# Four states of a selective scan through TensorE in the first three sequences, instead of two

## The chip, the cores and the metric

The kernel runs on one core of one Trainium2 chip. The metric is the device time of one execution, in microseconds (us). A core has five engines that run side by side and wait for each other by semaphores: TensorE (PE; its weight loads are listed as PEld), VectorE (DVE), ScalarE (ACT), GpSimd (POOL) and SyncE (SP), which here only issues DMAs. ACT also issues some DMAs.

## The reference

Sixteen sequences of 512 positions and 256 features go through a bidirectional state-space layer with a residual and a layer norm, and then through a soft mixture of 16 experts with a residual and a layer norm. The part that matters here is the scan. Per sequence and direction, with 512 channels and 16 states:

```
dA  = dt * A                      # per channel and state
dBu = dt * u * B                  # B: one value per position and state
xs  = recurrence h[t] = exp(dA[t]) * h[t-1] + dBu[t], with a gate for the reference's 1e-12
y   = sum over states of xs * C   # C: one value per position and state
y   = y + u * D, times silu(res)
```

The backward direction runs over the positions in reverse. `dt` is a softplus of a projection of `u`, and `B` and `C` are projections of `u` as well.

## The kernel before

**Layout.** Channels lie on the 128 partitions, in four chunks of 128, and the 512 positions along the free dimension. All is in fp32. For each sequence `b` the scan is done in four calls of `scan_part(b, r, p, ...)`: pair 0 of the chunks forward (`r` = 0) and backward (`r` = 1), then pair 1 forward and backward. I call these calls parts. Three sequences make twelve parts, numbered 0 to 11.

**One part** loops over the 16 states two at a time (`n` = 0, 2, ..., 14) and in it over the two chunks of the pair. That makes 16 steps, each with two states of one chunk. In a step:

- POOL multiplies `du` = dt*u with the broadcast rows `bs` of B into `db` (L427), for both states at once: 128 x 1024.
- ACT makes the decay exp(dt*A) into `h` in PSUM (L444) and a tanh gate `th` (L446), one of each per state.
- DVE runs the recurrence, one `tensor_tensor_scan` per state (L450 forward, L452 backward), and multiplies with the gate into `hg` (L455).
- POOL multiplies `hg` with the broadcast rows `cs` of C (L456), again 128 x 1024.
- PE adds `hg` into the accumulator `acc` in PSUM by matmuls with the identity (L371, in `add_up`), two steps late. `hg` has four buffers, `db`, `bs` and `cs` have three.

**Diagonal states.** For the two states in `DIAG` = (5, 13) the product dt*u*B is not made by POOL. PE makes it as a matmul of the transposed `du` (`duT`, turned by PE and copied by ACT in `turn_pair`, L350 and L355) with a matrix `dg` that has the row of B on its diagonal (L405, in `by_diagonal`). It issues four 128x128 matmuls per state and chunk, into a PSUM bank `hd`, one step ahead of the scan that reads it. In such a step `db` is only 128 x 512 (`k` = 1), half of `bs` is loaded, and the decay of the diagonal state goes to `dec` in SBUF.

**Where the diagonal matrices come from.** `diag_dram` holds one matrix per direction, diagonal state and group of 128 positions, in rows of P+1 elements, so that column 0 of that view is the diagonal. At the start the whole of it is zeroed from an SBUF tile `blank`, by DMAs on ACT's queue (L188). In `project_unit`, when `xd` (which holds the rows of B and C) is there, one DMA on ACT's queue writes the diagonal elements of the direction's states, one by one (L297). `scan_part` then loads `dg` (L420, one buffer) on SP's queue, two states (one `n`) before its first use.

**Order around the scan.** SP's queue carries `bs` (L416), `cs` (L417), `dg`, the inputs and the weights, in one order. Beside the scan three lists of generators, `prep`, `front` and `back`, emit other work: the projections of the next direction or sequence, the layer norm and the expert routing of the sequence before, and from sequence 3 on also the experts. `beside_scan` gives each of them at most a piece per step, as long as the PSUM banks in use (three of tag `mps`, of which a held `hd` takes one) allow it. The order on each engine is fixed when the program is built, partly by a scheduler and partly by `late`, which keeps an instruction at its place. The constants of the later stages are loaded by `constants`, called once after the first `prep_forward`.

Of the kernel before, what the change touches and what calls it, by code (L numbers as in the profile page):

```python
# [9 lines left out]
F32 = mybir.dt.float32  # L10
# [7 lines left out]
P = 128  # L18
L = 512
NL = L // P  # L20
# [4 lines left out]
NS = 16  # L25
DTR = 16
XB, XC = 32, 64
XW = XC + NS
KW = 4
NE = 16  # L30
DIAG = (5, 13)
DIAG_SIZE = P * (P + 1)
SL = 64
NSL = NE * SL
# [21 lines left out]
def seq_layers(tc, ident, neghalf, a, out):  # L56
# [20 lines left out]
    nc = tc.nc  # L77
    nb = a["x"].shape[0]
    with ExitStack() as ctx:
        drams = ctx.enter_context(tc.tile_pool(name="drams", bufs=1, space=DRAM))  # L80
# [2 lines left out]
        s_dram = drams.tile([nb, NM, P, NSL], F32, name="s_dram")  # L83
        e_dram = drams.tile([NE, nb * SL, DM], F32, name="e_dram")

        diag_dram = drams.tile([2, len(DIAG), NL, DIAG_SIZE], F32, name="diag_dram")
        const = ctx.enter_context(tc.tile_pool(name="m_const", bufs=1))
        p1 = ctx.enter_context(tc.tile_pool(name="m_p1", bufs=1))
        p2 = ctx.enter_context(tc.tile_pool(name="m_p2", bufs=2))
# [53 lines left out]
        side = [{}, {}]  # L143
# [14 lines left out]
        def steps(w, s, m):  # L158
            w["dtT"] = const.tile([DTR + 1, DI], F32, name=f"dtT_{s}")
            nc.sync.dma_start(w["dtT"][:DTR, :], a[f"dt_proj{m}T"])  # L160
            nc.sync.dma_start(w["dtT"][DTR : DTR + 1, :], a[f"dt_proj{m}_b"].unsqueeze(0))
            w["A"] = const.tile([P, ND, NS], F32, name=f"A_{s}")
            nc.sync.dma_start(w["A"], a[f"A{m}_log"].rearrange("(c p) n -> p c n", p=P))
            d = channels(a[f"D{m}"], f"D_{s}")
            w["diagD"] = const.tile([P, ND, P], F32, name=f"diagD_{s}")
            for c in range(ND):
                late(nc.vector.tensor_scalar(w["diagD"][:, c, :], ident, d[:, c : c + 1], None, ALU.mult))
# [5 lines left out]
            nc.vector.tensor_scalar(w["Ah"], w["A"], 0.5, None, ALU.mult)  # L173

        def constants():
            steps(side[0], "f", "")
            projections(side[1], "b", "_b")
            steps(side[1], "b", "_b")
            outT = const.tile([P, ND, DM], F32, name="outT")
            nc.sync.dma_start(outT, a["out_projT"].rearrange("(c p) o -> p c o", p=P))  # L180
            late(nc.vector.tensor_scalar(outT, outT, 0.5, None, ALU.mult))
            return outT

        projections(side[0], "f", "")
        blank = p2.tile([P, 4 * DM], F32, tag="W", name="blank", bufs=3)
        nc.vector.memset(blank, 0.0)
        for part in diag_dram.rearrange("r i l (p s) -> (r i) p l s", p=P):
            nc.scalar.dma_start(part, blank[:, : NL * (P + 1)].rearrange("p (l s) -> p l s", l=NL))  # L188

        def taps(dst, src, w, c, last):  # L190

# [71 lines left out]
        def prep_gate(b, fwd, out):  # L263
# [8 lines left out]
                late(nc.vector.scalar_tensor_tensor(res[:, c, :], res[:, c, :], 1.0, pp, ALU.add, ALU.mult))  # L272
            out["res"] = res

        def project_unit(b, r, out):

            w = side[r]
            q = f"{b}_{r}"
            yield GAP + 1
            px = bank(f"px_{q}")  # L280
            for c in range(ND):
                nc.tensor.matmul(
                    px[:XW, :], w["xT"][:, c, :], out["u"][:, c, :], start=(c == 0), stop=(c == ND - 1)
                )
            yield HOLD
            xd = p1.tile([XW, L], F32, tag=f"xd_{r}", name=f"xd_{q}")
            bc = dram.tile([2, NS, L], F32, tag="bc", name=f"bc_{q}")
            if r == 0:
                late(nc.scalar.activation(xd, px[:XW, :], AF.Identity, bias=unit))
            else:  # L290

                late(nc.scalar.activation(xd[: XB + NS, :], px[: XB + NS, :], AF.Identity, bias=unit[: XB + NS]))
                nc.scalar.copy(xd[XC:XW, :], px[XC:XW, ::-1])
            nc.sync.dma_start(bc[0], xd[XB : XB + NS, :])
            nc.sync.dma_start(bc[1], xd[XC:XW, :])
            step = DIAG[1] - DIAG[0]
            nc.scalar.dma_start(  # L297
                diag_dram[r].rearrange("i l (p s) -> i l p s", p=P)[:, :, :, 0],
                xd[XB + DIAG[0] : XB + NS : step, :].rearrange("i (l p) -> i l p", p=P),
            )  # L300
            out.update(xd=xd, bc=bc)

# [89 lines left out]
        def scan_part(b, r, p, v, accs, done, then):  # L392

            prep.drain()
            prep.gens += [[1, g] for g in [turn_pair(b, r, p, v)] + then]
            w = side[r]
            made = {}

            def by_diagonal(n, c):

                diags.append(count[0])
                made[n, c] = h = bank(f"hd_{b}_{r}_{n}_{c}")
                for lc in range(NL):
                    s = slice(lc * P, (lc + 1) * P)
                    ins = nc.tensor.matmul(h[:, s], v[c][3][:, s], dg[:, s], start=True, stop=True)  # L405
                    if lc == 0:
                        late(ins)

            chunks = (2 * p, 2 * p + 1)
            for n in range(0, NS, 2):  # L410
                q = f"{b}_{r}_{p}_{n}"
                k = 1 if n + 1 in DIAG else 2

                bs = p4.tile([P, 2, L], F32, tag="bs", name=f"bs_{q}")
                cs = p4.tile([P, 2, L], F32, tag="cs", name=f"cs_{q}")
                nc.sync.dma_start(bs[:, :k, :], v["bc"][0, n : n + k, :].unsqueeze(0).to_broadcast([P, k, L]))  # L416
                nc.sync.dma_start(cs, v["bc"][1, n : n + 2, :].unsqueeze(0).to_broadcast([P, 2, L]))  # L417
                if n + 3 in DIAG:
                    dg = p4.tile([P, L], F32, tag="dg", name=f"dg_{q}", bufs=1)
                    nc.sync.dma_start(  # L420
                        dg.rearrange("p (l s) -> p l s", l=NL),
                        diag_dram[r, DIAG.index(n + 3), :, : P * P].rearrange("l (p s) -> p l s", p=P),
                    )
                for c in chunks:
                    dt, rr, du = v[c][:3]
                    db = p4.tile([P, 2, L], F32, tag="db", name=f"db_{q}_{c}")
                    nc.gpsimd.tensor_tensor(  # L427
                        db[:, :k, :], du.unsqueeze(1).to_broadcast([P, k, L]), bs[:, :k, :], ALU.mult
                    )
                    hg = p4.tile([P, 2, L], F32, tag="hg", name=f"hg_{q}_{c}", bufs=4)  # L430
                    hs = {}
                    for j in range(2):
                        if j < k:
                            dec = h = ps_h.tile([P, L], F32, tag="h", name=f"h_{q}_{c}_{j}")
                            hs[j] = (h, dec, db[:, j, :])
                        else:
                            h = made.pop((n + j, c))
                            dec = p4.tile([P, L], F32, tag="dec", name=f"dec_{q}_{c}", bufs=2)
                            hs[j] = (h, dec, h)

                    ths = {}
                    for j in range(2) if k == 2 else (1, 0):
                        s = slice(n + j, n + j + 1)
                        nc.scalar.activation(hs[j][1], dt, AF.Exp, scale=w["A"][:, c, s])  # L444
                        ths[j] = p4.tile([P, L], F32, tag="th", name=f"th_{q}_{c}_{j}")
                        nc.scalar.activation(ths[j], rr, AF.Tanh, bias=LN_1E12 / 2, scale=w["Ah"][:, c, s])  # L446
                    for j in range(2):
                        (h, dec, add), th = hs[j], ths[j]
                        if r == 0:
                            nc.vector.tensor_tensor_scan(h, dec, add, 0.0, ALU.mult, ALU.add)  # L450
                        else:
                            nc.vector.tensor_tensor_scan(  # L452
                                h[:, ::-1], dec[:, ::-1], add[:, ::-1], 0.0, ALU.mult, ALU.add
                            )
                        nc.vector.scalar_tensor_tensor(hg[:, j, :], th, 1.0, h, ALU.add, ALU.mult)  # L455
                    nc.gpsimd.tensor_tensor(hg, hg, cs, ALU.mult)  # L456
                    pending.append(
                        (r == n == 0, n == 0, r == 1 and n == NS - 2, c, hg, accs, w, v["u"], f"acc_{q}_{c}", done)
                    )
                    evict()  # L460

                    nxt_n = n if c == chunks[0] else n + 2
                    if nxt_n + 1 in DIAG:
                        for x in sides:
                            x.take_up()
                        by_diagonal(nxt_n + 1, chunks[1] if c == chunks[0] else chunks[0])
                    beside_scan()
                    if k == 1:
                        diags.pop(0)
                    add_up(2)  # L470
# [625 lines left out]
```

## Time and profile before

| what | value |
|---|---|
| median of 3 runs | 5410.14 us (5405.57 to 5413.56) |
| the profiled execution | 5411.23 us, span 5409.4 us |
| granted TensorE clock, mean | 0.889 |
| PE busy over the span | 4331.1 us (80%) |
| DVE busy | 4559.7 us (84%) |
| ACT busy | 4087.2 us (76%) |
| POOL busy | 4732.1 us (87%) |
| DMA | 907.73 MB, mean 168 GB/s |

A row of the groups reads: line, engine, operation, out<-in by the program's names, shapes, number of instructions | busy us, mean ns of one | idle time of the engine just before them, and what ended most of it. A row of the windows reads: stretch of the span in us from its start, its length, busy us (number of instructions) of PE, PEld, DVE, ACT and POOL, the granted TensorE clock, the share of the DMA engines, and GB/s. A row of the timeline reads: start, length, engine, line, operation, out<-in, count, and in brackets the idle time before it with its releaser.

The first `db` of sequence 0 begins at 40.7 us, that of sequence 1 at 336.1, of sequence 2 at 635.0, and of sequence 3 at 935.2. From there on the experts run beside the scan.

### The profile page before, as it was taken

What the parts mean: (1) busy time and instruction counts of PE and PEld (TensorE: products, weight loads), DVE (VectorE), ACT (ScalarE), POOL (GpSimd) and SP (SyncE); (2) the same over time, 40 slices, a digit from 0 to 9 for tenths busy, and PEclk for the clock granted to TensorE, in tenths of its full rate; (3) what the DMA queues carried; (4) which work ended last, traced back from release to release, by engine and by line L of the source; (5) the groups of instructions that cost most, each with busy time, mean ns of one, the idle gap of its engine ahead of it and who ended that gap; (6) DMA issues with size and microseconds to landing.
All of it is one profiled execution on the core that took longest, in us unless ns stands there. A gap on an engine that the chain in (4) does not pass through costs nothing. (4 is left out here: it accounts for less than half of the span.)

```text
span 5409.4 us, 73721 instructions
## 1 busy us (share of the span) xinstructions
PE 4331.1 (80%) x24144; PEld 3390.0 (63%) x24145; DVE 4559.7 (84%) x6276; ACT 4087.2 (76%) x6515; POOL 4732.1 (87%) x2537
## 2 busy tenths in 40 slices
PE   5656666898888978788888977889787897888889
PEld 3445555676666666677656765667656776667657
DVE  7888988889898899888998888988899889988722
ACT  6677777787888778887877887788788887877641
POOL 6999999999999899998999989998999989988600
PEclk7778778898899988899888989899889998989999
DMA  4334333575446644566446754467444764457436
GB/s 137 131 117 137 125 129 131 189 230 159 156 142 212 225 149 148 158 223 213 131 144 194 232 170 153 132 212 232 149 149 146 225 224 134 145 179 234 126 103 188
DMA packets 595236, 907.73 MB, mean 168 GB/s; under 512 B 78082, under 2 KB 384898, under 8 KB 594852
## 3 DMA queue, kind: packets, MB, share of 16 engines
q1 hardware_dynamic: 521156, 859.87, 49.5%
q10 hardware_dynamic: 73696, 43.14, 2.8%
q8 instruction: 192, 3.15, 0.2%
q14 instruction: 192, 1.57, 0.1%
HBM read 840.86 MB, written 62.01 MB: 167 GB/s over the span
## 5 line engine op out<-in xcount | busy, mean ns | idle before, releaser
L456 POOL TENSOR_TENSOR hg<-hg,cs 128x1024 f32<-128x1024 f32 x1024 | 2420.8, 2368 | 128.1 <-DVE hg L455 110.0
L427 POOL TENSOR_TENSOR db<-du,bs 128x1024 f32<-128x1024 f32 (+1 forms) x1024 | 2144.4, 2098 | 232.3 <-DVE h L450 84.7
L371 PE MATMUL acc<-ident,hg 128*128 128x128 f32 x8192 | 1179.3, 295 | 203.3 <-POOL hg L456 181.6
L455 DVE SCALAR_TENSOR_TENSOR hg<-th,h 128x512 f32<-128x512 f32 x1792 | 1185.8, 678 | 177.2 <-PE acc L371 90.4
L371 PEld LDWEIGHTS acc<-ident,hg 128*128 128x128 f32 x8192 | 1044.9, 154 | 390.8 <-POOL hg L456 240.9
L452 DVE TENSOR_TENSOR_SCAN h<-h,db 128x512 f32<-128x512 f32 x896 | 1072.8, 1218 | 112.2 <-ACT h L444 107.5
L450 DVE TENSOR_TENSOR_SCAN h<-h,db 128x512 f32<-128x512 f32 x896 | 1071.1, 1217 | 48.8 <-ACT h L444 45.7
L446 ACT ACTIVATE th<-rr,Ah_f 128x512 f32<-128x512 f32 x1024 | 725.0, 714 | 186.3 <-DVE hg L455 183.1
L446 ACT ACTIVATE th<-rr,Ah_b 128x512 f32<-128x512 f32 x1024 | 721.5, 712 | 155.2 <-DVE hg L455 147.7
L444 ACT ACTIVATE h<-dt,A_f 128x512 f32<-128x512 f32 x896 | 608.2, 680 | 117.5 <-DVE hg L455 112.6
L444 ACT ACTIVATE h<-dt,A_b 128x512 f32<-128x512 f32 x896 | 608.6, 681 | 108.8 <-DVE hg L455 105.1
L687 PE MATMUL pl<-x2T,seT 128*128 128x512 f32 x512 | 299.1, 715 | 78.7 <-DVE hg L455 37.4
L405 PE MATMUL hd<-dg,duT 128*128 128x128 f32 x2048 | 305.6, 298 | 32.7 <-ACT yt L627 13.5
L830 PEld LDWEIGHTS pg<-st,Wg 128*128 128x128 f32 x2048 | 244.8, 196 | 106.2 <-issue 85.0
L405 PEld LDWEIGHTS hd<-dg,duT 128*128 128x128 f32 x2048 | 283.1, 214 | 38.4 <-ACT yt L627 15.7
L806 PE MATMUL peo<-Wd,ht 128*128 128x256 f32 x1024 | 257.0, 407 | 55.6 <-DVE rr L337 38.6
L779 PE MATMUL pu<-st,Wu 128*128 128x128 f32 x2048 | 254.5, 283 | 50.1 <-DMA Wu<-in_Wu_dram 32.7
L962 PE MATMUL cpo<-ceo,ct 128*128 128x256 f32 x1024 | 254.8, 407 | 46.9 <-DVE rr L337 39.9
L779 PEld LDWEIGHTS pu<-st,Wu 128*128 128x128 f32 x2048 | 244.9, 198 | 61.5 <-DVE h L452 24.2
L830 PE MATMUL pg<-st,Wg 128*128 128x128 f32 x2048 | 269.9, 286 | 4.1 <-DMA Wg<-in_Wg_dram 3.1
L884 PE MATMUL cl<-seT,cx 128*128 128x512 f32 x512 | 244.7, 617 | 32.5 <-DVE res L272 12.3
L806 PEld LDWEIGHTS peo<-Wd,ht 128*128 128x128 f32 x1024 | 205.3, 206 | 97.7 <-DVE rr L337 41.2
(154 smaller groups left out, 6654.8 us busy)
## 6 DMA issues: line engine op xcount, KB each, us to landing
cs<-bc SPq DMA_DIRECT2D x512, 512.0 KB, 3.9
bs<-bc SPq DMA_DIRECT2D x384, 512.0 KB, 5.1
Wg<-in_Wg_dram SPq DMA_DIRECT2D x128, 512.0 KB, 6.0
Wu<-in_Wu_dram SPq DMA_DIRECT2D x128, 512.0 KB, 6.0
Wd<-in_Wd_dram SPq DMA_DIRECT2D x128, 512.0 KB, 5.5
dg<-diag_dram SPq DMA_DIRECT2D x128, 256.0 KB, 4.2
bs<-bc SPq DMA_DIRECT2D x128, 256.0 KB, 3.6
x<-in_x_dram SPq DMA_DIRECT2D x32, 512.0 KB, 6.3
```

Of the source, the lines that this page charges most:

```text
L371: ins = nc.tensor.matmul(accs[c][:, s], hc[:, j, s], ident, is_transpose=True, start=False, stop=(last and j == 1 and lc == NL - 1),)
L405: ins = nc.tensor.matmul(h[:, s], v[c][3][:, s], dg[:, s], start=True, stop=True)
L427: nc.gpsimd.tensor_tensor(db[:, :k, :], du.unsqueeze(1).to_broadcast([P, k, L]), bs[:, :k, :], ALU.mult)
L444: nc.scalar.activation(hs[j][1], dt, AF.Exp, scale=w["A"][:, c, s])
L446: nc.scalar.activation(ths[j], rr, AF.Tanh, bias=LN_1E12 / 2, scale=w["Ah"][:, c, s])
L450: nc.vector.tensor_tensor_scan(h, dec, add, 0.0, ALU.mult, ALU.add)
L452: nc.vector.tensor_tensor_scan(h[:, ::-1], dec[:, ::-1], add[:, ::-1], 0.0, ALU.mult, ALU.add)
L455: nc.vector.scalar_tensor_tensor(hg[:, j, :], th, 1.0, h, ALU.add, ALU.mult)
L456: nc.gpsimd.tensor_tensor(hg, hg, cs, ALU.mult)
L779: nc.tensor.matmul(pu[:, fc * P : (fc + 1) * P], got["Wu", e][:, k, fc * P : (fc + 1) * P], st[:, k, :, j * SL : (j + 1) * SL], start=(k = ...
L806: nc.tensor.matmul(po[:, j * DM : (j + 1) * DM], ht[:, fc, :], got["Wd", e0 + j][:, fc, :], start=(fc == 0), stop=(fc == NF - 1),)
L830: nc.tensor.matmul(pg[:, fc * P : (fc + 1) * P], got["Wg", e][:, k, fc * P : (fc + 1) * P], st[:, k, :, j * SL : (j + 1) * SL], start=Fals ...
```

## The change

In the sequences 0, 1 and 2 the diagonal states are (3, 7, 11, 15) instead of (5, 13). From sequence 3 on they stay (5, 13). `diag_dram` has room for four states per direction. The zeroing of the forward direction's four matrices stays where it was; that of the backward direction's four is written at the head of `constants`. The column write of `project_unit` covers the states of the sequence at hand.

```diff
-DIAG = (5, 13)
+DIAGS = 4
...
-        diag_dram = drams.tile([2, len(DIAG), NL, DIAG_SIZE], F32, name="diag_dram")
+        diag_dram = drams.tile([2, DIAGS, NL, DIAG_SIZE], F32, name="diag_dram")
...
         def constants():
+            blanks(1)
             steps(side[0], "f", "")
...
-        for part in diag_dram.rearrange("r i l (p s) -> (r i) p l s", p=P):
-            nc.scalar.dma_start(part, blank[:, : NL * (P + 1)].rearrange("p (l s) -> p l s", l=NL))
+        def blanks(r):
+            for part in diag_dram[r].rearrange("i l (p s) -> i p l s", p=P):
+                nc.scalar.dma_start(part, blank[:, : NL * (P + 1)].rearrange("p (l s) -> p l s", l=NL))
+
+        blanks(0)
...
+        def diag_of(b):
+            return (3, 7, 11, 15) if b < 3 else (5, 13)
...
-            step = DIAG[1] - DIAG[0]
+            ds = diag_of(b)
             nc.scalar.dma_start(
-                diag_dram[r].rearrange("i l (p s) -> i l p s", p=P)[:, :, :, 0],
-                xd[XB + DIAG[0] : XB + NS : step, :].rearrange("i (l p) -> i l p", p=P),
+                diag_dram[r, : len(ds)].rearrange("i l (p s) -> i l p s", p=P)[:, :, :, 0],
+                xd[XB + ds[0] : XB + NS : ds[1] - ds[0], :].rearrange("i (l p) -> i l p", p=P),
             )
...
-                k = 1 if n + 1 in DIAG else 2
+                k = 1 if n + 1 in ds else 2
...
-                if n + 3 in DIAG:
+                if n + 3 in ds:
                     dg = p4.tile([P, L], F32, tag="dg", name=f"dg_{q}", bufs=1)
                     nc.sync.dma_start(
                         dg.rearrange("p (l s) -> p l s", l=NL),
-                        diag_dram[r, DIAG.index(n + 3), :, : P * P].rearrange("l (p s) -> p l s", p=P),
+                        diag_dram[r, ds.index(n + 3), :, : P * P].rearrange("l (p s) -> p l s", p=P),
                     )
...
-                    if nxt_n + 1 in DIAG:
+                    if nxt_n + 1 in ds:
```

More of the change, by code (lines that the diff above doesn't have):

```diff
@@ L395, in scan_part @@
             prep.gens += [[1, g] for g in [turn_pair(b, r, p, v)] + then]
-            w = side[r]
+            w, ds = side[r], diag_of(b)
             made = {}
```

## The prediction

> **What bounds the kernel now.** The change acts on the first three of sixteen sequences, so the page's averages (POOL 87%, DVE 84%) don't decide it. I read first the times at which POOL starts each sequence's first `db` product (L427). They cut the span: start-up to 40.7 us, part 0 (the first sixteen steps) to 115.5, parts 1 to 11 to 935.2, then one sequence after another. Busy time in these windows (length, then PE, PEld, DVE, ACT, POOL busy with instructions, granted clock, DMA share, GB/s):
>
> ```profile
> 0.00:40.70 40.70, 22.31 (x40) 8.31 (x40) 16.28 (x34) 13.37 (x17) 3.96 (x15) 0.85 0.72 160
> 40.70:115.50 74.80, 36.09 (x161) 27.10 (x162) 72.45 (x89) 55.74 (x88) 68.91 (x40) 0.66 0.42 130
> 115.50:935.20 819.70, 538.20 (x2767) 422.96 (x2767) 712.49 (x862) 607.46 (x958) 802.08 (x413) 0.77 0.39 128
> ...
> 1259.30:1565.00 305.70, 244.60 (x1305) 186.81 (x1305) 280.25 (x383) 243.83 (x405) 292.97 (x157) 0.89 0.46 143
> 1565.00:1897.80 332.80, 284.88 (x1717) 229.05 (x1716) 286.16 (x399) 266.51 (x410) 297.72 (x158) 0.93 0.65 208
> ```
>
> In parts 1 to 11 POOL is busy 802.1 of 819.7 us (97.9%), DVE 712.5 (87%), PE 66%, ACT 74%: POOL sets the pace there. Part 0 is another case: DVE is busy 72.45 of 74.8. Next, the groups by shape inside 115 to 935 us:
>
> ```profile
> L456 POOL TENSOR_TENSOR hg<-hg,cs 128x1024 f32<-128x1024 f32 x177 | 420.9, 2382 | 0.4 <-DVE hg L455 0.4
> L427 POOL TENSOR_TENSOR db<-du,bs 128x1024 f32<-128x1024 f32 x132 | 314.6, 2387 | 3.0 <-issue 1.7 <-POOL hg L456 1.3
> ...
> L427 POOL TENSOR_TENSOR db<-du,bs 128x512 f32<-128x512 f32 x44 | 57.0, 1296 | 13.4 <-DVE h L452 13.4
> ...
> L452 DVE TENSOR_TENSOR_SCAN hd<-dec,hd 128x512 f32<-128x512 f32 x24 | 29.2, 1219 | 39.5 <-PE hd L405 39.5
> ```
>
> Nearly all of POOL is `db` (two states, 2387 ns; one state, 1296 ns) and `hg`. The last row shows DVE waiting 39.5 us for the PE product `hd`. I take that for back-pressure: the `hd` matmuls stand on PE behind an accumulation that waits for POOL's `hg` (L371 waits for L456 in the waits of that stretch), and POOL hardly pauses. The two waits of 7 to 8 us among them, in parts 5 and 9, did reach POOL: they are most of the 13.4 us above. Last, the timeline of the start:
>
> ```profile
> 2.22 5.90 ACTq L188 DMA_DIRECT2D diag_dram<-blank  x4
> ...
> 8.15 1.28 ACT L230 ACT_TABLE_LOAD   x1 [8.15 <-DMA diag_dram<-blank]
> ```
>
> ACT's first work stands behind the four zeroing DMAs; the fourth is issued at 7.75 us, when the first has landed.
>
> **What the Trainium skill says.** GPSIMD Engine Reference (3.1 Elementwise) gives an fp32 `tensor_tensor` of 2048 elements as 4497 ns, 2.2 ns per element; here the second 512 elements cost 2387 - 1296 = 1091 ns, 2.13 each, so the trace agrees that half a `db` is nearly half its price. DMA: Bandwidth & Descriptors (Rules for kernel authors) says that a non-contiguous last dimension lowers to one descriptor per element. The trace fits: the column DMA L297 moves 4 KB, yet is issued at 34.97 us and the load behind it (L420) gets off only at 46.81. Perfetto Trace Analysis (Optimization Strategy) says that a kernel can have regimes with different most-contended engines; the windows above show that.
>
> **The change, part by part.**
>
> *POOL loses work.* Each of the twelve parts (three sequences, two directions, two pairs of channel chunks) gets four diagonal states instead of two, for two chunks: four more `db` products of half width, 48 in all, 44 in parts 1 to 11. 44 x 1.091 = 48.0 us. POOL then needs 802.1 - 48.0 = 754.1 us there. In part 0, where DVE is full, I count its 4.4 us as nothing.
>
> *How much of it reaches the end.* DVE does not change (scan of `hd` 1219 ns against 1218 of `h`), so DVE to POOL becomes 712.5 / 754.1 = 0.945, and the two must mesh more tightly. The trace has such a stage: 1259 to 1565 us, DVE 280.25 to POOL 292.97, 0.957, with PE and ACT fuller than here. Its span is 305.70 / 292.97 = 1.043 of POOL. 754.1 x 1.043 = 786.9, so 819.7 - 786.9 = **33 us gained**. Bounds: POOL keeps today's 17.6 us of idle time, 48 gained; or the stages go like the crowded one after it (332.80 / 297.72 = 1.118 of POOL), 843, 23 lost.
>
> *PE gains work.* A group of four `hd` matmuls is 58.2 / 44 = 1.32 us; 48 x 1.32 = 63 us, PE going from 66% to about 76% of the stretch. It lies beside POOL. New is the place: state 3 is used at the third step of a part, so its first group follows the turned `du` (L350, L355) closely. In the trace of before the copy of `duT` ends 2.6 to 9.9 us before the scan that would use it in parts 1 to 11 (ends 874.4 for a scan at 877.7 in part 11), and the group takes 1.3. Counted as nothing; if that cover is gone it is a piece of the crowded bound.
>
> *ACT.* A decay into `dec` is 712 ns against 680 for `h`: 48 x 0.03 = 1.5 us on an engine with 26% idle: nothing.
>
> *SP and the DMAs.* 24 more `dg` loads of 256 KB, 24 `bs` loads of 512 KB halved: the bytes are equal. SP gets 24 issues of 0.39 us, 9 us in 890: nothing. `dg` keeps one buffer, so a load waits for PE's previous group and holds `bs` and `cs` behind it; but `cs` ahead of it already waits for an `hg` of about the same step, so SP runs no less far ahead.
>
> *Zeroing, eight DMAs instead of four.* The second four are written later in the source, but they depend on nothing that would keep them there: in the changed program's order all eight stand on ACT's queue ahead of the table load at 8.15 us. The fifth to eighth wait in turn for loads of the start and for the third zeroing (landed about 10.6 us); the fourth landed at about 13. So the table load comes between 11 and 15 us. I take 12.7: **4.5 us lost** (2 to 7) on the chain ACT, PE, DVE that fills the first 40 us. SP's start-up loads share the completion semaphores with these DMAs and slip alike.
>
> *The column write of the start.* It has 2048 elements instead of 1024, and is now read for state 3, so its `dg` load stands on SP ahead of the second `bs` (before: behind it). The old one took up to 11.8 us; I estimate 14 to 18, which puts the second `bs` some 20 us after `xd`, where POOL wants it 12 to 15 after. POOL stalls perhaps 7 us, DVE, the bound of part 0, 2 to 3: **3 us lost** (0 to 8). Later column writes are issued 24 to 30 us ahead of their part and are covered.
>
> *From sequence 3 on* every engine's order is the same as before: nothing.
>
> Sum: -33 + 4.5 + 3 = -25.5 us on the profiled execution's 5411.2 (span 5409.4). That execution is 1.1 above the median of the runs, 5410.1, so I predict 5384.
>
> **The rivals.**
>
> *A, the saving arrives nearly whole.* For it: POOL at 98%, and in the stage at 0.957 DVE waits for `hd` only 3.1 us in 305.7. Parts 1 to 11 gain 43 to 48, the start costs 2 to 4: 5364 to 5371.
>
> *B, the start and the coupling eat it.* PE-side stalls such as the 6.3 us ones of parts 5 and 9 grow (`hd` behind the transposes of the layer norm), the gain falls to 12 or less and the start costs 10: within 11 us of before, 5399 to 5421.
>
> *C, slower: DVE waits for PE at every diagonal state.* Today it waits (39.5 + 13.2) / 44 = 1.2 us per `hd`. Were that PE's own lateness and not POOL's pressure, DVE would need 712.5 + 88 x 1.2 = 818 us, plus what else it waits for (some 50), about 860 against 819.7: 40 slower, 5450. It decides from about (819.7 - 712.5 - 50) / 88 = 0.65 us per `hd`. Against it: 0.2 us per `hd` in the stage from 1259 us, where the same code runs with PE fuller.
>
> *D, it does nothing:* excluded, since the halved products are in the changed program and POOL is the bound.
>
> **How the numbers follow.** The main case (5372 to 5398) has 0.58, A 0.22, B 0.13, C 0.07. Main and A are faster by more than 0.2% (11 us, about what a measurement of this kernel can tell from no change): 0.80. B is the same, 0.13; C slower, 0.07. The range leaves out C and the upper half of B: 5362 to 5408.
>
> **What would show it.** In the changed profile: 88 half products in parts 1 to 11 near 1290 ns, POOL busy about 754 us there, and the stretch near 787; the first ACT table load at 11 to 15 us; the first `db` of part 0 at about 45 us; waits for `hd` under 0.5 us each; sequence 3 to the end as long as before. POOL's share under 92% in those parts would break the step on meshing; a `hd` wait above 0.65 us that POOL does not cause would make C right.

## The result and the profile after

The changed kernel takes 5363.24 us (median of 4 runs, 5360.15 to 5368.92) against 5411.73 for the kernel before in the same measurement. The ratio is 0.9914, with a 95% interval of 0.9896 to 0.9931. The profiled execution took 5362.05 us (span 5360.1) and is compared here with the one before (span 5409.4).

First the windows of the changed kernel, cut at the same events as before: start-up, part 0, parts 1 to 11, then the sequences 4 and 5. The columns are those of the windows above.

```profile
0.00:45.00 45.00, 23.89 (x42) 9.12 (x43) 16.45 (x35) 13.79 (x19) 4.01 (x15) 0.83 0.81 169
45.00:116.20 71.20, 40.85 (x194) 32.17 (x193) 70.50 (x88) 52.91 (x81) 64.44 (x39) 0.69 0.43 129
116.20:889.90 773.70, 545.60 (x3107) 443.71 (x3106) 708.89 (x860) 606.90 (x959) 755.37 (x414) 0.82 0.44 136
...
1213.40:1519.50 306.10, 245.33 (x1307) 187.71 (x1307) 280.35 (x383) 243.72 (x405) 292.87 (x157) 0.88 0.46 143
1519.50:1847.00 327.50, 281.20 (x1704) 226.04 (x1703) 284.92 (x397) 266.04 (x409) 297.57 (x158) 0.93 0.67 212
```

Read the second numbers, the lengths. Start-up is 4.3 us longer (40.7 to 45.0), part 0 is 3.6 shorter (74.8 to 71.2), parts 1 to 11 are 46.0 shorter (819.7 to 773.7), and the two later sequences stand within some us of 305.7 and 332.8. Sequence 3 starts 45.3 us earlier and sequence 15 46.5. POOL's busy time in parts 1 to 11 is 755.37 us, where 754.1 was predicted. The groups by shape of the changed kernel, in the same stretch:

```profile
L465 POOL TENSOR_TENSOR hg<-hg,cs 128x1024 f32<-128x1024 f32 x177 | 418.2, 2365 | 9.2 <-DVE hg L464 9.1
...
L436 POOL TENSOR_TENSOR db<-du,bs 128x1024 f32<-128x1024 f32 x89 | 210.6, 2368 | 6.5 <-issue 3.9 <-DVE h L461 1.9 <-POOL hg L465 0.6
...
L436 POOL TENSOR_TENSOR db<-du,bs 128x512 f32<-128x512 f32 x88 | 112.3, 1278 | 1.7 <-DVE h L461 1.7
...
L461 DVE TENSOR_TENSOR_SCAN hd<-dec,hd 128x512 f32<-128x512 f32 x46 | 55.9, 1215 | 6.8 <-PE hd L414 4.3 <-ACT th L455 2.6
```

There are 88 half products (44 before), and the half that is saved is 2368 - 1278 = 1090 ns, or 2.13 ns for each of its 512 elements; the Trainium skill's GPSIMD Engine Reference (3.1 Elementwise) gives 2.2. Two idle times differ from the rows of before: the halved `db` waited 13.4 us for a scan of DVE and waits 1.7 now, and the scan of `hd` waited 39.5 us for PE and waits 4.3 now. With the scans of the forward direction (4.3 too) that is 8.6 us for 88 uses, 0.1 each instead of 1.2. Last, the timeline of the start:

```profile
2.22 9.76 ACTq L191 DMA_DIRECT2D diag_dram<-blank  x8
12.01 1.28 ACT L235 ACT_TABLE_LOAD   x1 [12.01 <-DMA diag_dram<-blank]
...
38.81 1.25 ACTq L306 DMA_DIRECT2D diag_dram<-xd  x1
...
48.45 0.37 SPq L429 DMA_DIRECT2D dg<-diag_dram  x1
...
53.10 2.50 POOL L436 TENSOR_TENSOR db<-du,bs 128x512 f32<-128x512 f32 x2 [3.37 <-DMA bs<-bc]
```

All eight zeroing DMAs stand ahead of ACT's first work, which begins 3.9 us later (8.15 to 12.01). The column write is out of the way 9.6 us after its issue, and POOL then waits 3.37 us for the `bs` that stands behind the `dg` load on SP.

### The profile page after: what moved, and what is told of

Same layout as the page of the kernel before. It is cut to its first block, busy times and chain, and to the rows that moved or that the text cites. A ratio compares the mean times of both kernels' runs of the same rounds, so it can differ in the third digit from the quotient of the medians.

```text
span 5360.1 us, 74569 instructions
## 1 busy us (share of the span) xinstructions
PE 4327.5 (81%) x24529; PEld 3402.3 (63%) x24529; DVE 4556.1 (85%) x6276; ACT 4086.3 (76%) x6515; POOL 4680.7 (87%) x2537
## 5 line engine op out<-in xcount | busy, mean ns | idle before, releaser
L436 POOL TENSOR_TENSOR db<-du,bs 128x1024 f32<-128x1024 f32 (+1 forms) x1024 | 2090.0, 2045 | 229.1 <-DVE h L459 82.3
L464 DVE SCALAR_TENSOR_TENSOR hg<-th,h 128x512 f32<-128x512 f32 x1744 | 1159.5, 681 | 179.1 <-PE acc L380 96.1
L380 PE MATMUL acc<-ident,hg 128*128 128x128 f32 x8192 | 1161.7, 291 | 106.9 <-POOL hg L465 85.1
L380 PEld LDWEIGHTS acc<-ident,hg 128*128 128x128 f32 x8192 | 1033.1, 152 | 287.0 <-POOL hg L465 126.7
L461 DVE TENSOR_TENSOR_SCAN h<-h,db 128x512 f32<-128x512 f32 x872 | 1046.0, 1221 | 110.3 <-ACT h L453 101.4
L459 DVE TENSOR_TENSOR_SCAN h<-h,db 128x512 f32<-128x512 f32 x872 | 1045.5, 1221 | 48.7 <-ACT h L453 48.0
L453 ACT ACTIVATE h<-dt,A_f 128x512 f32<-128x512 f32 x872 | 591.5, 680 | 100.8 <-DVE hg L464 97.7
L453 ACT ACTIVATE h<-dt,A_b 128x512 f32<-128x512 f32 x872 | 592.2, 680 | 86.1 <-DVE hg L464 82.3
L414 PE MATMUL hd<-dg,duT 128*128 128x128 f32 x2432 | 369.4, 301 | 73.3 <-ACT duT L364 28.2
L414 PEld LDWEIGHTS hd<-dg,duT 128*128 128x128 f32 x2432 | 341.5, 217 | 83.6 <-ACT duT L364 30.4
```

The source lines that it names most:

```text
L380: ins = nc.tensor.matmul(accs[c][:, s], hc[:, j, s], ident, is_transpose=True, start=False, stop=(last and j == 1 and lc == NL - 1),)
L436: nc.gpsimd.tensor_tensor(db[:, :k, :], du.unsqueeze(1).to_broadcast([P, k, L]), bs[:, :k, :], ALU.mult)
L461: nc.vector.tensor_tensor_scan(h[:, ::-1], dec[:, ::-1], add[:, ::-1], 0.0, ALU.mult, ALU.add)
```

## The experiments

Where a kernel has a line or two more than the changed one, its line numbers are higher by that. Lengths of parts and sequences are taken between first `db` products. They come from one execution each. Four of the kernels below do the same in parts 1 to 11 (the zeroing held back, four states in the first three sequences); they took 768.9 to 771.6 us there, which shows how far such a length repeats.

### The start: hold the zeroing back, or give it to another queue

Theory: the start is ACT's first table load, which waits for eight zeroing DMAs. In the first kernel `blanks(1)` is called just ahead of the setup of the expert stage and each of its DMAs is kept at its place; in the second all eight go to POOL's queue.

```diff
-            blanks(1)
...
+        blanks(1)
         front.add(8, moe_setup())
...
+                if r == 1:
+                    late(ins)
...
-                nc.scalar.dma_start(part, ...)
+                nc.gpsimd.dma_start(part, ...)
```

> The changed kernel, with the backward direction's four zeroing DMAs held behind the first decays in ACT's queue, so that four instead of eight stand ahead of ACT's first table load. Theory (the eight zeroing DMAs at the head cost the start 4.3 us, which nothing gives back): the table load comes back to 8.2 us, POOL's first db to about 41 us, parts 1 to 11 stay near 774 us, and the whole is about 4 us below the changed kernel, 5359. Rival (the delay is only moved: the four zeroing DMAs now run beside the first loads of bs and cs and hold those up): first db at 41, but part 0 longer by about 4, and the whole within 1 us of the changed kernel, 5363.

> The changed kernel, with all eight zeroing DMAs issued from POOL's queue, where POOL has nothing to do until 42 us. Theory (ACT's wait for the zeroing is what delays the start, and the DMA work itself is beside it): ACT's table load falls to about 1 us and its first copy to about 7 us (13.3 in the changed kernel), the first db comes at 38 to 40 us, and the whole is 5 to 7 us below the changed kernel, about 5357. Rival (the start is bound by the DMA engines and SP's loads, not by ACT): first db at 43 to 45 as in the changed kernel, the whole within 1 us of it.

With the zeroing held back the table load comes at 8.61 us and the first `db` at 41.9, 3.1 us earlier. But part 0 takes 73.8 us instead of 71.2, so part 1 starts only 0.5 us earlier. POOL's third `db` of part 0 waits 7.85 us, where it waited 3.37 in the changed kernel:

```profile
54.45 2.50 POOL L437 TENSOR_TENSOR db<-du,bs 128x512 f32<-128x512 f32 x2 [7.85 <-DVE hg L465]
```

In the three other kernels with the zeroing held back and four states in the first sequence this wait is 6.3 to 7.7 us, for the load of `bs`. So for the start the rival is right in the main: the delay moves into part 0. Sequence 3 nevertheless starts at 885.6 us instead of 889.9, because parts 1 to 11 took 769.9 us instead of 773.6; why they are shorter is open. And the whole took 5365.7 us, ratio 0.9914 [0.9899, 0.9929], no less than the changed kernel: sequence 15 also starts 4.4 us earlier, and the last stage (all from there on) is 8.8 us longer. In the windows from the first `db` of sequence 15 to the last `db`, first of this kernel, then of the changed one, the scan's work is the same:

```profile
4695.30:5068.70 373.40, 316.80 (x1807) 253.14 (x1806) 286.58 (x417) 268.56 (x422) 291.03 (x152) 0.90 0.58 186
```

```profile
4699.70:5065.50 365.80, 305.88 (x1816) 245.84 (x1816) 286.12 (x417) 268.28 (x421) 290.81 (x152) 0.94 0.60 190
```

DVE, ACT and POOL are busy equally long, but PE's granted clock is 0.90 against 0.94 and PE is busy 10.9 us longer. The last stage of kernels that differ only in the first three sequences varied between 660.4 and 675.8 us. So a few us at the start can't be read from the whole time of this kernel, only from the windows.

With POOL's queue the table load comes at 0.73 us and yet the first `db` only at 46.2: PE waited 13.0 us for a `w_pin` load that SP issued late. Freed from ACT, the start is bound by SP's loads. Part 0 was 68.9 and parts 1 to 11 770.8, so that sequence 3 starts at 885.9, as early as with the zeroing held back, though the first `db` came 4.3 us later than there; the whole took 5369.7, ratio 0.9922 [0.9907, 0.9936].

### Is it POOL's work, or PE's?

One kernel keeps the four products of PE but lets POOL make every `db` in full; another keeps POOL's halves but leaves out PE's products in the first three sequences.

```diff
+                kb = 2 if b < 3 else k          # POOL in full: bs and db of width kb
...
-                        if j < k:
+                        if j < k or b < 3:      # no product by PE
```

> The changed kernel with PE's hd products of four states, but in the first three sequences POOL makes the full db product of both states all the same (the half for the diagonal state is made and not read). So POOL's saving is taken away and PE's added work stays. Theory (POOL is the bound and PE's work lies beside it): parts 1 to 11 about 820 us as before the change, hd waits of DVE back at about 1 us each or more, the whole 4 us above the kernel before (the start), 5412 to 5420. Rival (PE's hd chain costs time of its own, and the change's saving is net of it): parts 1 to 11 at 840 us or more, the whole 5435 or more.

> The changed kernel, but in the first three sequences no hd products and no dg loads are made: the scan of the diagonal state reads the other state's half of db (left out: dt*u*B of states 3, 7, 11 and 15 there). So POOL's saving stays and PE's added work goes. Theory (PE's work is covered): parts 1 to 11 within 5 us of the changed kernel's 774, the whole 5358 to 5365. Rival (PE's chain eats part of the saving): parts 1 to 11 at 760 or less, the whole 5350 or less.

POOL in full: 5453.99 us, ratio 1.0078 [1.0061, 1.0095], parts 1 to 11 at 850.9. The expectation was set wrongly: it took this kernel to have POOL's work of before, but before had two halved states and this one has none. Counted rightly, POOL has 88 halves more than in the changed kernel, 755.4 + 88 x 1.09 = 851.3 us, and the window shows it filled to the last us:

```profile
123.90:974.80 850.90, 581.04 (x3115) 467.06 (x3115) 712.22 (x861) 608.59 (x959) 849.98 (x413) 0.79 0.44 137
```

Without PE's products parts 1 to 11 take 775.7 us, no less than the 773.7 with them, and the whole 5373.11, ratio 0.9927 [0.9912, 0.9942]. PE's added work is covered. (Without the products the decays go to PSUM as well, so this kernel differs in more than PE's work.)

### POOL's work of before, in two ways

Now the right comparison: four states by PE, but POOL's amount of before (states 3 and 11 get an unused full product).

```diff
+                kb = 2 if b < 3 and n + 1 in (3, 11) else k
```

> The changed kernel, but in the first three sequences two of its four diagonal states (3 and 11) still get a full db product of POOL, whose second half nobody reads: TensorE makes four products as in the changed kernel, POOL works as much as in the kernel before. Theory (the gain is POOL's alone, and TensorE's added groups cost nothing): parts 1 to 11 go back from 773.7 to 773.7 + 44 x 1.09 = 821.6, within 3 us, and the whole to about 5410. Rival (the added groups of TensorE or the new states' places take something of their own, which the changed kernel's lighter POOL hides): parts 1 to 11 at 830 or more, the whole at 5420 or more.

It took 5405.8 us, ratio 0.9998 [0.9989, 1.0007]. Parts 1 to 11 came to 806.6 us, neither the theory's 821.6 nor the rival's 830: **13 us of the change's 46 don't come from POOL's lighter load.** The whole does not show them: in the profiled executions sequence 3 starts 9.6 us earlier than in the kernel before, and the interval of the ratio allows a gain of 6 us at most. The next kernel is the better witness for the whole. The window and POOL's waits in it (waiter, releaser, us in total, times, longest):

```profile
119.00:925.60 806.60, 566.51 (x3111) 455.61 (x3110) 709.42 (x859) 606.51 (x957) 802.57 (x413) 0.80 0.44 137
```

```profile
POOL hg L466 <- DVE hg L465: 2.1, 2, 1.0
POOL db L437 <- DVE h L462: 1.0, 2, 0.8
```

POOL works the same 802 us as before (802.08) but has 4 us of idle time instead of 17.6. The difference lies in parts 3, 5 and 9, which took 76.1, 79.7 and 80.3 us before and take 72.3, 76.2 and 76.1 here. In part 5 of the kernel before, these lines of the timelines of ACT, PE, DVE and POOL belong together, in order of time:

```profile
424.63 0.60 ACT L607 ACTIVATE x<-x,m_sh,m_rs 128x256 f32<-128x256 f32 x1 [7.60 <-POOL m_sh L602]
430.75 1.97 PE L371 MATMUL acc<-ident,hg 128*128 128x128 f32 x8 [7.18 <-POOL hg L456]
432.51 1.92 PE L384 MATMUL acc<-diagD_b,xb 128*128 128x128 f32 x8
434.21 1.10 PE L405 MATMUL hd<-dg,duT 128*128 128x128 f32 x8
435.43 1.23 DVE L452 TENSOR_TENSOR_SCAN hd<-dec,hd 128x512 f32<-128x512 f32 x1 [7.18 <-PE hd L405]
439.78 1.27 POOL L427 TENSOR_TENSOR db<-du,bs 128x512 f32<-128x512 f32 x1 [5.54 <-DVE h L452]
...
445.10 1.09 PE L668 MATMUL px<-ident,xn 128*128 128x128 f32 x4 [8.00 <-DVE res L272]
```

ACT waits 7.60 us for the layer norm's shift `m_sh`, which POOL makes, and the next decays stand behind it on ACT, so DVE runs dry and POOL's next `hg` comes late. On PE the `hd` of state 5 stands behind the accumulation that waits for this `hg`. DVE waits for `hd`, and POOL in the end 5.54 us for DVE. Part 9 goes the same way (7.06 for ACT, 7.96 for DVE, 6.32 for POOL). The layer norm's transposes `px` wait too, but until 445.10, when POOL is at work again: in the rest of part 5 POOL has no pause of 0.5 us or more. So they are not what held up this `hd`. Is it the places of the states among such pieces of side work that removed the stalls, or the number of products by PE? The next kernel has two states, as before, at other places:

```diff
-            return (3, 7, 11, 15) if b < 3 else (5, 13)
+            return (7, 15) if b < 3 else (5, 13)
```

> The changed kernel with two diagonal states in the first three sequences as before the change, but at 7 and 15 instead of 5 and 13; POOL has the same work as in the kernel before and as in the run in which POOL works as before (806.6 us for parts 1 to 11, where the kernel before takes 819.7). Theory (the 13 us between those two come from where the states stand among the pieces of side work on PE's queue, which moves the layer norm's transposes px away from a waiting hd): parts 1 to 11 at 803 to 811, none of them over 77, and no wait of DVE for hd above 4 us. Rival (it is the four products themselves, whose decays go to SBUF and leave PSUM's banks free, that remove the stalls): 816 to 822, with parts of 79 to 80 again.

Parts 1 to 11 took 808.6 us (POOL 802.44), none over 77.0, so the places account for 11 of the 13 us; the other 2 are no more than parts 1 to 11 of equal programs differ by. In part 5 ACT waits for `m_sh` as before, but the next `hd` on PE comes much later:

```profile
425.21 0.60 ACT L616 ACTIVATE x<-x,m_sh,m_rs 128x256 f32<-128x256 f32 x1 [7.31 <-POOL m_sh L611]
444.04 1.06 PE L414 MATMUL hd<-dg,duT 128*128 128x128 f32 x8
```

POOL has one pause above 0.5 us in this part, of 0.55. So the theory's range came about, and what the states moved away from is the moment at which ACT waits for the layer norm, not the transposes that the theory names. Its detail on `hd` missed: DVE still waited once 11.7 us for one (in part 1), but POOL had no wait above 2.2. The whole was 5403.93, ratio 0.9985 [0.9979, 0.9992].

### How far does a lighter POOL carry?

Two doses beyond the change: `db` is of half width in two more, or in all, of the four values of `n` that still have full products. Both kernels leave out the product of the second state there.

```diff
+                kb = 1 if b < 3 and n in (4, 12) else k     # or in (0, 4, 8, 12)
...
-                            hs[j] = (h, dec, db[:, j, :])
+                            hs[j] = (h, dec, db[:, min(j, kb - 1), :])
```

> The changed kernel, but in the first three sequences two of the four steps without a diagonal state (n = 4 and 12) use the db product of their first state for both states: it leaves out the second state's product there, 44 halves in parts 1 to 11 less for POOL, 755.4 - 48 = 707.4 us, as much as DVE's 708.9. Nothing else changes but the bytes of bs. Theory (POOL's idle time of some 18 us stays what it is until DVE has no slack left): POOL + 18 = 725, and DVE's own 709 with the few us that it waits come to the same; 722 to 735. Rival 1 (two engines at equal load mesh worse, in the proportion 1.043 that the prediction took from the stage at 0.957): 709 x 1.043 = 740 or more, up to 755. Rival 2 (something else than POOL sets parts 1 to 11 by now): 765 to 774.

> As the one with half of them, but in all four steps without a diagonal state (n = 0, 4, 8, 12) of the first three sequences: every db product there has half width, POOL is down to 755.4 - 96 = 659.4 us in parts 1 to 11, and DVE with 708.9 is alone at the top. It leaves out the second state's product in those steps. Theory (DVE is the next bound, and runs as full as in part 0, 70.5 of 71.2): 715 to 728. Rival (PE or the handing over between the engines bounds at 1.043 of DVE or more): 740 to 755. In both the second half of the dose brings much less than its 48 us: under 20.

Parts 1 to 11 took 760.6 and 758.5 us, so no range of either expectation was met, only the common one that the second half of the dose brings under 20 us (it brought 2.1); the wholes were 5352.71, ratio 0.9897 [0.9883, 0.9912], and 5352.15, ratio 0.99 [0.9885, 0.9915]. The windows tell why. First the kernel with all four steps halved, then the changed kernel; the rows are parts 1 to 3, sequence 1 and sequence 2:

```profile
111.70:302.50 190.80, 132.44 (x780) 107.47 (x778) 183.74 (x216) 152.75 (x236) 178.60 (x109) 0.81 0.42 130
302.50:586.80 284.30, 205.54 (x1156) 168.57 (x1157) 263.03 (x325) 227.32 (x362) 242.11 (x153) 0.82 0.40 121
586.80:870.10 283.30, 206.75 (x1174) 170.34 (x1173) 261.66 (x323) 227.06 (x362) 242.05 (x153) 0.83 0.40 123
```

```profile
116.20:320.80 204.60, 136.90 (x781) 112.36 (x779) 185.99 (x217) 154.80 (x240) 203.96 (x109) 0.80 0.44 138
320.80:604.40 283.60, 203.23 (x1159) 164.80 (x1160) 261.05 (x322) 225.00 (x359) 275.75 (x154) 0.83 0.44 137
604.40:889.90 285.50, 205.48 (x1169) 166.55 (x1168) 261.85 (x323) 227.10 (x362) 275.66 (x154) 0.83 0.43 134
```

In sequence 0 POOL fills the changed kernel (203.96 of 204.60), and less work for it still shortens the parts, to 190.8 with DVE at 183.7. In sequences 1 and 2 a POOL lighter by 33.6 us brings nothing in one and 2 us in the other: POOL is not the bound there any more. DVE is busy 263 of 284 us, and its remaining pauses are short waits for several engines, ACT's decays first: 17.9 us in these two sequences, and 18.0 in the changed kernel. There the change already took all that POOL had to give. That DVE with these waits sets the pace there is read from the numbers; no run makes DVE lighter.

### More states: in all sequences, and in the first

Both kernels have the zeroing held back. One makes `diag_of` return (3, 7, 11, 15) for all sequences. The other has six states in sequence 0 and keeps `dg` per state:

```diff
+            return (3, 5, 7, 9, 11, 13) if b == 0 else (3, 7, 11, 15) if b < 3 else (5, 13)
...
-                    dg = p4.tile([P, L], F32, tag="dg", name=f"dg_{q}", bufs=1)
+                    dg = p4.tile([P, L], F32, tag="dg", name=f"dg_{q}", bufs=2)
```

> Four diagonal states in all sixteen sequences instead of the first three; the zeroing of the backward matrices is held back behind the first decays of the backward direction. From sequence 3 on POOL has 16 half products less in each, 17.4 us, TensorE 16 groups more, 21 us. Theory (the lighter engine POOL lets go what it held): the even sequences, 306 us with POOL at 293 and DVE at 280, go to 290 to 297; the odd ones, 329 us with POOL at 298 and PE at 281, gain less, 318 to 330; the whole 5230 to 5320. Rival (beside the experts and combines PE's work and the meshing of the engines decide, the lower bound that the prediction took for parts 1 to 11): even sequences 303 or more, odd ones 330 to 345; the whole 5350 to 5480.

> Six diagonal states (3, 5, 7, 9, 11, 13) in sequence 0, four in sequences 1 and 2, two after, with two dg buffers and, to make room, two cm buffers instead of three. Four zeroed forward matrices are written by ACT's queue and two by POOL's; the backward ones are held back behind the first decays. Theory (only sequence 0 is still bound by POOL, since the runs with half products of the other steps went from 275.8 to 260.2 and 257.9 us there and not at all in sequences 1 and 2): sequence 0 at 258 to 266, sequences 1 and 2 at 283 as before, sequence 3 starting at 866 to 874, the whole at 5345 to 5356. Rival (with a diagonal state at every step two hd products stand ahead in PSUM, and PE or the side work fails to keep up): sequence 0 at 272 or more and the whole at 5360 or more.

**Four everywhere** is slower: 5668.84 us, ratio 1.0482 [1.0466, 1.0498], well beyond the rival's range. The first such sequence, 3, gains 13 us (309.5 against 322.5), but sequence 4 takes 331.9 and sequence 6 339.4, and the stage after the last scan grows. The window after the last `db`, of this kernel and of the changed one:

```profile
5200.50:5665.00 464.50, 428.20 (x2220) 323.31 (x2220) 124.55 (x337) 139.96 (x256) 31.07 (x59) 0.97 0.54 165
```

```profile
5065.50:5360.10 294.60, 261.37 (x1338) 194.90 (x1335) 81.91 (x215) 88.75 (x174) 28.09 (x54) 0.97 0.45 140
```

PE has 2220 instructions left there instead of 1338: experts and combines that did not fit beside the scans are done at the end, alone (twice as many matmuls of the experts' `pg` and `pu` as in the changed kernel, 512 each instead of 256). Between them the sequences are longer although no engine is fuller (POOL 278, DVE 280, PE 263 of sequence 4's 331.9). That the side work is kept out because `hd` holds PSUM banks is how the program's rule reads; I did not test it by itself. A kernel with four states in sequences 0 to 3 only, which would have shown whether sequence 3's gain is lost again later, gave no result: its program deadlocks.

**Six in sequence 0**: 5370.28 us, ratio 0.9922 [0.9909, 0.9936]. Parts 1 to 3 gained 10.3 us against the kernel with the zeroing held back (204.0 to 193.7), as the theory wants, but the first `db` came at 46.9 and part 0 took 79.8 instead of 73.8. The timeline of POOL and of SP's queue there:

```profile
45.30 1.54 POOL L190 DMA_DIRECT2D diag_dram<-blank  x2
...
63.95 2.49 POOL L438 TENSOR_TENSOR db<-du,bs 128x512 f32<-128x512 f32 x2 [12.45 <-DMA bs<-bc]
```

```profile
56.13 0.37 SPq L431 DMA_DIRECT2D dg<-diag_dram  x1
56.55 0.50 SPq L426 DMA_DIRECT2D bs<-bc  x1
```

The column write has 3072 elements here, and six zeroing DMAs run beside it: four of ACT's queue, and the two that I gave to POOL's queue, at 45.3 us. The `dg` load came 7.7 us later than in the changed kernel, and POOL waited 12.45 us for the `bs` behind it. In numbers the rival came about (sequence 0 took 273.6 us, the whole 5370.28), but not for its reason: in parts 1 to 3 DVE waits 0.7 us for `hd`, and the loss lies mainly before and in part 0. So this run doesn't tell what six states are worth with a clean start; it does show the chain column write, `dg`, `bs`, POOL that the prediction described.

### The places in the later sequences

Since places were worth 11 us in the first sequences, the last two kernels move the two states of the sequences from 3 on; the first three keep four, with the zeroing held back.

```diff
-            return (3, 7, 11, 15) if b < 3 else (5, 13)
+            return (3, 7, 11, 15) if b < 3 else (3, 11)     # or (5, 11)
```

> Four states in the first three sequences, and in the later ones two as before the change, but at 3 and 11 instead of 5 and 13; zeroing of the backward matrices held back behind the first decays. Theory (places among the side work matter there too, where POOL is busy 293 of 306 us): the even sequences from 4 on change by 3 us or more, the odd ones too, in either direction, the whole by 30 us or more against 5365.7. Rival (the places matter only where the layer norm meets them, in the first sequences): all within 2 us of 306 and 329, the whole within 10 us of 5365.7.

> As the run with the later places at 3 and 11, but at 5 and 11: the first state at its old place, only the second moved. Theory (the loss of that run comes from state 3, whose first group on PE follows the turned du closely and keeps the side work's pieces out): the even sequences at 304 to 308 to the end, the whole within 10 us of 5365.7. Rival (any other place than 5 and 13 lets fewer pieces of side work in, so that they pile up until the last stage): the even sequences grow to 312 or more from sequence 6 on, the whole at 5400 to 5460.

With (3, 11): 5459.02 us, ratio 1.0088 [1.0072, 1.0105]; the sequences 8 to 14 take 318 to 322 and 334 to 336 us instead of 306 to 308 and 329. With (5, 11): **5351.3 us, ratio 0.9886 [0.9872, 0.9899], the lowest median of the full kernels**. The even sequences grow to 314 as the rival had it and the odd ones shrink from 329 to 317 as nobody had it, so that sequence 15 starts at 4678.6 us instead of 4695.3. The first of the two met its theory, that the places matter there too; the whole of the second missed both ranges. The interval of (5, 11) just touches that of (5, 13), [0.9899, 0.9929], so the gain of the whole is small against its noise; the loss of (3, 11) is not. POOL's work is equal in all of them (590.7 to 591.0 us in sequences 8 and 9 together for (3, 11) and (5, 13), 590.7 for (5, 11)). So the places alone change how long the even and the odd sequences take; why (3, 11) loses and (5, 11) wins is open.

## Why the prediction was right or wrong

The direction and the bound were right; the size was not, 48.5 us instead of 25.5. The measured 5363.24 lies at the lower edge of the stated range (5362 to 5408) and outside the main case (5372 to 5398). Rival A's 43 to 48 us in parts 1 to 11 came about, but not for its reason: 11 to 13 of the 46 us came from the states' places and not from POOL's saving. A's whole, 5364 to 5371, was missed by 0.8 us, since the start and part 0 together lost 0.7 us and not 2 to 4.

| step | predicted | measured |
|---|---|---|
| POOL busy in parts 1 to 11 | 754.1 | 755.4 |
| length of parts 1 to 11 over POOL's busy time | 1.043 | 1.024 |
| parts 1 to 11 | -33 | -46.0 |
| of that, by POOL's halves | -33 | -32.9 (806.6 to 773.7) |
| of that, by the states' places | not counted | -11 to -13 |
| part 0 with the column write | +3 | -3.6 |
| zeroing at the start | +4.5 | +4.3 |
| sequences 3 to 14 | 0 | -1.2 |
| sequence 15 to the end | 0 | -2.8 |

**POOL's halves** were priced rightly. That their share came to within 0.1 us of the forecast is partly luck: the step used one factor, 1.043, for the whole stretch. In truth parts 1 to 3 took over 12.4 us (217.0 to 204.6) of the 12 x 1.09 = 13.1 that were there, and sequences 1 and 2 20.5 (589.6 to 569.1) of about 35, because there DVE, by the windows, takes over. A factor from another stage stood for two stages with different bounds.

**The missing 13 us** are the step that failed: the factor on meshing, 1.043, which let POOL's idle time grow from 17.6 us to 32.8. It was 18.3. The prediction read the waits of DVE for `hd` rightly, as back-pressure through the accumulation that waits for POOL, and saw that those in parts 5 and 9 reached POOL and made up most of 13.4 us of its idle time. It kept this idle time and did not ask whether it belonged to the places of the states, which the change moves. It did: at equal work POOL's idle time shrank to 4 and 6 us at the new places, and only the lighter load brought it back to 18.3. (The split into places and halves holds in this order; no run has the lighter POOL with the states at 5 and 13.)

**Part 0** failed in two terms. "DVE is full, so POOL's 4.4 us count as nothing" took DVE's 97% for a bound. Among the kernels with all zeroing DMAs at the head of ACT's queue, part 0 took 74.5 with POOL's work of before, 71.2 with the halves, and 68.0 and 67.1 with still more halves: POOL's work did count. DVE's busy time in part 0 fell too, from 72.45 us before the change to 64.82 in the kernel with the lightest POOL, at nearly the same number of instructions. Of these 7.6 us, 6.5 lie in six small instructions, which last as long as POOL's products beside them (last section): a busy share that contains such time is no bound. And the column write was mis-sized: 9.6 us instead of 14 to 18. Before, four loads of `bs` and `cs` were issued between the write and the `dg` load, now two; that these loads made up much of the 11.8 us of before fits, but no run shows it by itself. POOL waited 3.4 us for `bs`, not 7.

**The start** was right in mechanism and size up to the first `db`; that such a delay reaches the end was assumed, and the kernel with the zeroing held back shows that most of it is made up in part 0. **PE's added work** was costed at nothing, rightly: without it parts 1 to 11 took 775.7 us. ACT's and SP's additions were not tried by themselves; no run shows a cost. **Sequence 3 on** was right, but the last stage moves by several us with the granted clock.

**Rival C** is refuted: DVE waits 0.1 us per `hd`, where the stage from 1259 us of the profile before had suggested 0.2. (Its sum was also 8 us short: 818 and 50 are 868, not 860.) **Rival B** did not occur, and its picture of `hd` behind the layer norm's transposes is not what part 5 of the kernel before shows. The bound of 1.118 did not apply to the first three sequences; four states in all sequences show that a loss of this kind is real once experts run beside the scan.

## What to carry to other kernels

- Split a stretch until each piece has one bound, and cut the gain off in each piece where the next engine takes over; a factor taken over the whole hides that.
- When a step moves, look at what stands in front of it on its engine's queue and how late that is, before and after. Here the same amount of work at other places moved parts 1 to 11 by 11 us, and the whole by 93 us up or 14 down when the places of the later sequences were changed.
- Work given to an engine with slack is not free everywhere because it is free in one stage: four states in all sixteen sequences were 300 us slower than four states in the first three, where no experts run beside the scan.
- Before a full engine is called the bound, look for instructions in its busy time that take far longer than their size explains.

## What was unexpected of the hardware

**Small DVE instructions that take as long as a POOL product.** First two rows of DVE in part 0 for the same instruction, before and after the change, then two lines of the timeline before:

```profile
L171 DVE TENSOR_SCALAR A_b<-A_b 128x64 f32<-128x64 f32 x1 | 2.4, 2381 | 0.0
```

```profile
L171 DVE TENSOR_SCALAR A_b<-A_b 128x64 f32<-128x64 f32 x1 | 0.2, 182 | 0.0
```

```profile
83.32 2.40 DVE L559 TENSOR_SCALAR slot_b<-slot_b,scale 128x2 f32<-128x2 f32 x1
83.33 2.36 POOL L427 TENSOR_TENSOR db<-du,bs 128x1024 f32<-128x1024 f32 x1
```

An instruction on 128 x 2 elements took 2.4 us and ended when POOL's product ended. In eight of the kernels here 23 of these small `TENSOR_SCALAR` instructions took 1.1 to 5.3 us around part 0, and each ended within 0.07 us after a POOL product; the others took about 0.2 us. Only the coincidence is shown, not what holds them.

**The last stage and the clock.** Kernels with the same order of instructions from sequence 3 on differed by up to 15 us in the last stage alone (660.4 to 675.8). Part of that goes with the granted clock: from the first to the last `db` of sequence 15, six of them took 365.8 to 369.1 us at a clock of 0.92 to 0.94, and five 370.2 to 373.4 at 0.90 to 0.91. The Trainium skill's TensorE: Matmul & The Clock Gate (Part 1: The HAM clock gate) says that the clock drops to half when activity pauses and is judged in windows of about 3.4 us. The clock records of the changed kernel and of the one with the zeroing held back agree with that: in the last stage their spells at 0.5 are 3.4 or 6.8 us long, but for the one at the end, and fall at other times in each. What starts a spell at one place and not at another is open.
